# A four-layer transformer on one core: when the rows of layer 1's experts are listed and gathered, and where the first score maxima are kept

## The chip, the cores and the metric

The kernel runs on one core of one Trainium2 chip. A core has five engines with instruction streams of their own: TensorE (PE in the profile) for matmuls and transposes, VectorE (DVE), ScalarE (ACT), GpSimd (POOL), and SyncE (SP), which issues DMAs. TensorE writes into PSUM, a small memory that VectorE and ScalarE read, but GpSimd does not. The metric is the device time of one execution in microseconds (us), as the median of several runs; smaller is better.

## The reference

Four layers, each an attention and a feed-forward part, work on 16 sequences of 256 tokens, 128 features each (4096 tokens). Around each part stands a layer norm with a scale and a shift per sequence, and its output is added to the stream `x` with a gate per sequence. The change touches layer 1's feed-forward part and, by a shared routine, layer 2's attention. Layer 1's feed-forward part is itself a small transformer layer, with attention over 16 heads of 8 features and a mixture of 8 experts, of which each token uses two:

```python
def _L1_ffn_ref(src, ...):
    x = _ln(src + _attention(src, Wq, bq, Wk, bk, Wv, bv, Wo, bo), ln1_g, ln1_b)
    gates = softmax(x @ gW + gb)
    top2_scores, top2_idx = top_k(gates, 2)
    w = (one_hot(top2_idx, 8) * top2_scores[..., None]).sum(1)
    h = relu(einsum('nd,edf->enf', x, W1) + b1[:, None, :])
    y = einsum('enf,efd->end', h, W2) + b2[:, None, :]
    return _ln(x + einsum('ne,end->nd', w, y), ln2_g, ln2_b)
```

Layer 2's attention has 16 heads of 8 features too, rotary positions, and a causal mask. Both are softmax attentions: for each query the largest score is subtracted from the scores ahead of the exponential.

## The kernel before, in words

All of `x` stays in SBUF, features on partitions. Tokens are worked on in 8 blocks of 512 (two sequences).

**The attention of heads of 8** (`attend8`) is used by layer 1's feed-forward part and by layer 2's attention. A unit is one sequence; a block has two units, and a unit has `per` = 8 cycles. In a cycle TensorE makes scores of one sort for a later unit, queries by keys, from which only the maxima are taken (`Sm`, in the PSUM place `ps_max`; VectorE's reduction at L1343 reads them), and scores of the other sort for the current unit, keys by queries, of which ScalarE takes the exponential (`Se`, in `ps_exp`; L1348). Each of the two places holds one tile. The maxima run `lead` = 10 cycles ahead (`per + self.LEAD`). So in the first ten cycles of each call there are maxima and no exponentials: `live_e` is false, `ps_exp` stands unused, and each cycle's scores have to wait until VectorE has read those before. When the eight maxima of a unit are there, `less_maxima` turns them and takes them from the queries (`qm`, L1236).

The maxima use keys multiplied with a mask (`km`, L1224, two instructions on GpSimd). They are made by `start_unit`, at the end of the last cycle of the unit ahead; `mt` counts the cycles of a unit's maxima, and `mt == per - 1` is the last.

**Later work.** At the end of each cycle `self.advance()` takes one step of each generator in `self.later`. In layer 1 these are `gates(blk)`, one for each finished block. It makes the gate's softmax and then chooses: the two best experts of each token (`top1` twice) with the one-hot rows, the weights, and then `listed`. Blocks choose in groups: `{1: (0, 1), 3: (2, 3), 5: (4, 5), 6: (6,), 7: (7,)}`: block 5's generator does blocks 4 and 5 together.

**Lists.** The 4096 tokens are handled as two halves of four blocks. For each half there is an array `rows` in device memory with a list for each expert. `listed` counts, by matmuls, the place of each token in the lists of its two experts, and then for each block turns its 512 tokens to rows (`list_rows`) and writes them to their places by 8 indirect DMAs from GpSimd (128 rows of 128 numbers each, L819). With a half's last block `pieces` works out which expert each piece of 256 rows belongs to.

**Pieces.** After the attention a loop runs over 2 x 23 pieces. `fetch` loads a piece's rows and the expert's weights (L1530 and L1532, from SP's queue), `turn` turns the rows, `hidden` and `out` do the expert's two layers, and the result goes to `done` in device memory (L1564, from ScalarE's queue). Step n of the loop does `fetch(n + 2)`, `turn(n)`, `hidden(n - 1)`, `out(n - 2)` and then three times `self.advance()`. The second half's pieces read the second half's lists.

**Tails.** When the first half's results are out (step 24), `tail(0)` starts among the later work: for each block 8 indirect DMAs on GpSimd fetch both experts' results of each token back from `done` (L1476); then it yields a fixed number of steps, `9 if self.in_pieces else 4`, adds the biases by matmuls, sums the two gathered rows with their weights on VectorE (8 instructions), turns the sum back on TensorE (`sums_turned`), and ends with a layer norm and the addition to `x`. A tail starts the next one when its own gathers are issued. Two buffers serve the gathered rows, so tail 2 waits until tail 0 has summed. Tails 0 to 3 run among the second half's pieces, tails 4 to 7 in layer 2's attention.

**The order.** In these stages TensorE's instructions keep the order in which the program writes them (`self.strict`). The streams of the other engines are put in order by a planner at build time: among the instructions that it takes for ready, by its own costs and due times, it takes the one written first; what it takes for ready early may move far ahead. So memory fills that layer 2 writes stand among layer 1's list DMAs in the trace. On the chip each engine then goes through its stream in that order and waits at each instruction for what that instruction needs.

Of the kernel before, what the change touches and what calls it, by code (L numbers as in the profile page):

```python
# [9 lines left out]
F32 = mybir.dt.float32  # L10
# [221 lines left out]
class _Kernel:  # L232
    def __init__(self, ctx, tc, t, out):
        self.ctx, self.tc, self.nc, self.t, self.out = ctx, tc, tc.nc, t, out
        self.turn = 0
        self.strict = self.strict_all = False
        self.later = []
        self.in_pieces, self.listed_halves, self.tailed, self.holds = False, 0, 0, {}
        self.tails_begun = self.halves_done = self.summed = 0
        self.lists_on = False  # L240
        self.dve, self.act, self.gps = (_InOrder(self, e) for e in (tc.nc.vector, tc.nc.scalar, tc.nc.gpsimd))


# [536 lines left out]
    def listed(self, blks, src, chosen, pool):  # L780

        half, t0 = divmod(4 * blks[0], 16)
        n = 4 * len(blks)
        ts = slice(t0, t0 + n)
        H, ends = self.hots[half][:, :, ts], self.ends[half]
        ps = self.bank()
        pv = ps[:, : 8 * (n + 1)].rearrange("p (t e) -> p t e", e=8)
        self.mm(pv[:, :n], self.prefix, chosen, start=True, stop=False, skip_group_check=True)
        for t in range(n):
            self.mm(  # L790
                pv[:, t + 1 :], self.c("mean"), bc(chosen[:, t : t + 1], [P, n - t, 8]),
                start=False, stop=t == n - 1, skip_group_check=True,
            )
            if t % 4 == 3:
                yield True
        at = pool.tile([P, n, 8], F32, tag="l_at", name="l_at")
        self.dve.scalar_tensor_tensor(at, pv[:, :n], float(P), bc(ends.unsqueeze(1), [P, n, 8]), ALU.mult, ALU.add)
        self.dve.scalar_tensor_tensor(ends, pv[:, n], float(P), ends, ALU.mult, ALU.add)
        yield
        z = self.list_z[:, :, :n]  # L800
        for i in range(2):
            self.dve.tensor_mul(z[:, i], H[:, i], at)
        yield
        place = self.place[half][:, :, ts]
        self.dve.tensor_reduce(place, z, AX.X, ALU.add)
        idx = pool.tile([P, 2, n], I32, tag="l_i", name="l_i", bufs=2)
        self.dve.tensor_copy(idx, place)
        for k, blk in enumerate(blks):
            ps = self.bank()
            for t in range(4):  # L810
                self.turned(ps[:, t * P : (t + 1) * P], src[:, blk * BLK + t * P : blk * BLK + (t + 1) * P])
            yield True
            rows = self.list_rows[:, blk % 4, :]
            self.act.copy(rows, ps)
            yield
            for t in range(4):
                for i in range(2):
                    to = bass.IndirectOffsetOnAxis(ap=idx[:, i, 4 * k + t : 4 * k + t + 1], axis=0)
                    self.nc.gpsimd.indirect_dma_start(self.rows[half][:, :], to, rows[:, t * P : (t + 1) * P], None)  # L819
                    if not self.in_pieces or i:  # L820
                        yield
        if blks[-1] % 4 == 3:
            yield from self.pieces(half, pool)
# [353 lines left out]
    def attend8(self, nt, group, prepare, finish, scale, causal=False, masks=(None, None)):  # L1177
# [124 lines left out]
        for cycle in range(-lead, units * per):  # L1302
            mx, ex = cycle + lead, cycle
            mu, mt = divmod(mx, per)
            eu, et = divmod(ex, per)
            live_m, live_e = mu < units, ex >= 0
            if mx == 0:
                start_unit(0)
            mms = []
            if live_m:  # L1310
                cs, t, j0 = first[mt]
                nk = (t + 1) * P if causal else NQ
                d = U[mu]
                Sm = self.ps_max.tile([P, 1024], F32, tag="max", name="ps_max").rearrange("p (j c i k) -> p j c i k", j=2, c=len(cs), i=2)
                if qmask is not None:
                    for j in range(2):
                        o = Sm[:, j, :, :, nk - P : nk].rearrange("p c i k -> p (c i) k")
                        self.mm(o, self.ident16, bc(qmask.unsqueeze(1), [P, 2 * len(cs), P]), skip_group_check=True)
                for c in range(len(cs)):
                    for j in range(2):  # L1320
                        r = slice(32 * (j0 + j), 32 * (j0 + j) + 32)
                        mms.append((c, Sm[:, j, c, :, :nk], d["q"][r, cs[c], t * P : (t + 1) * P], d["km"][r, cs[c], :, :nk], qmask is None and c == 0))
            if live_e:
                xcs, xt, xj0 = then[et]
                q0 = xt * P if causal else 0
                e = U[eu]
                Se = self.ps_exp.tile([P, 1024], F32, tag="exp", name="ps_exp").rearrange("p (j c i q) -> p j c i q", j=2, c=len(xcs), i=2)
                if kmask is not None:
                    for j in range(2):
                        o = Se[:, j].rearrange("p c i q -> p (c i) q")  # L1330
                        self.mm(o, self.ident16, bc(kmask.unsqueeze(1), [P, 2 * len(xcs), P]), skip_group_check=True)
                for c in range(len(xcs)):
                    for j in range(2):
                        r = slice(32 * (xj0 + j), 32 * (xj0 + j) + 32)
                        mms.append((c, Se[:, j, c, :, q0:], e["k"][r, xcs[c], xt * P : (xt + 1) * P], e["qm"][r, xcs[c], :, q0:], kmask is None and c == 0))
            for c, o, lhsT, rhs, fresh in sorted(mms, key=lambda x: x[0]):
                self.mm(o, lhsT, rhs, start=fresh, skip_group_check=True)
            if live_m:

                a = self.m8[mu % 2][:, t, 8:9]  # L1340
                dims = [list(a.ap[0]), [32, 2], [2 * P, len(cs)], [P + 16, 2]]
                o = bass.AP(tensor=a.tensor, offset=a.offset + 2 * P * cs[0] + 32 * j0, ap=dims)
                nc.vector.tensor_reduce(o, Sm[:, :, :, :, :nk], AX.X, ALU.max, negate=True)  # L1343
            if live_e:
                if xj0 == 0:
                    e["E"] = self.att.tile([P, 4, len(xcs), 2, NQ], F32, tag="E8", name="E8", bufs=3)
                E = e["E"][:, xj0 : xj0 + 2, :, :, q0:]
                nc.scalar.activation(E, Se[:, :, :, :, q0:], AF.Exp, scale=scale)  # L1348
                if causal:
                    D = e["E"][:, xj0 : xj0 + 2, :, :, q0 : q0 + P].rearrange("p j c i q -> p (j c i) q")  # L1350
                    nc.gpsimd.affine_select(D, D, [[0, 4], [1, P]], ALU.is_ge, 0.0, base=0, channel_multiplier=-1)
            for f in held:
                f()
            held = []
            if live_m and mt == per - 1:
                held.append(lambda u=mu: less_maxima(u))
            if live_e and et == 0:
                held.append(lambda u=eu: values(u))
            if live_e and xj0 == 2:
                held.append(lambda u=eu, x=et, E=e["E"]: weighted(u, x, E))  # L1360
            sides = [g for g in sides if step(g)]
            self.advance()
            for g in ready.values():
                step(g)

            if live_m and mt == per - 1 and mu + 1 < units:
                start_unit(mu + 1)
        for f in held:
            f()
        for g in sides:  # L1370
# [6 lines left out]
    def layer1_ffn(self):  # L1377
# [21 lines left out]
        with ExitStack() as ctx:  # L1399
# [4 lines left out]
            def gates(blk):  # L1404
# [3 lines left out]
                yield  # L1408
                yield from self.gate_softmax(comb[:, 4 * blk : 4 * blk + 4, :], 4, 8, one)
                yield  # L1410
                blks = {1: (0, 1), 3: (2, 3), 5: (4, 5), 6: (6,), 7: (7,)}.get(blk)
                if not blks:
                    return
                n = 4 * len(blks)
# [50 lines left out]
            def tail(blk):  # L1465
# [5 lines left out]
                g = self.list_rows[:, 2 * (blk % 2) : 2 * (blk % 2) + 2, :].rearrange("p a (u i d) -> p (a u) i d", i=2, d=P)  # L1471
                wT, acc = self.h1[:8, :], sums[:, blk % 2, :]
                for t in range(4):
                    for i in range(2):
                        of = bass.IndirectOffsetOnAxis(ap=self.origin[half][:, i, t0 + t : t0 + t + 1], axis=0)
                        nc.gpsimd.indirect_dma_start(g[:, t, i], None, self.done[half][:, :], of)  # L1476
# [2 lines left out]
                self.tails_begun = blk + 1  # L1479
                if blk + 1 < 4 * self.halves_done:  # L1480
                    self.later.append(tail(blk + 1))
                for _ in range(9 if self.in_pieces else 4):
                    yield
                ps = self.bank()
                for t in range(4):
# [6 lines left out]
                for i in range(2):  # L1492
                    for t in range(4):
                        v = slice(t * P, (t + 1) * P)
                        self.dve.scalar_tensor_tensor(
                            acc[:, v], g[:, t, i], w[:, i, t0 + t : t0 + t + 1], acc[:, v] if i else ps[:, v], ALU.mult, ALU.add
                        )
                    yield
                self.summed = blk + 1
                y = self.sums_turned(acc)  # L1500
# [630 lines left out]
```

## Time and profile before

| | us |
|---|---|
| median of 3 runs (lowest to highest) | 3432.42 (3426.85 to 3433.61) |
| the profiled execution's own time | 3416.51 |
| its span, first to last instruction | 3414.8 |
| layer 1, attention of heads of 8: first maxima | from 1789.7 |
| its first exponentials' cycle | 1826.0 |
| its last exponential (L1348) begins | 2238.4 |
| first half's pieces end on TensorE | 2312.3 |
| second half's pieces on TensorE | 2339.0 to 2419.3 |
| layer 2's attention: first maxima | 2450.5 |

Busy shares of the span: PE 90%, DVE 58%, ACT 51%, POOL 37%; the mean granted TensorE clock is 0.946. In a timeline each line is one instruction, or several alike in a row (x2): start, busy time, engine, source line, operation, output from input, and in brackets how long the engine stood idle ahead of it and what ended the wait. In lists of waits a line says which engine waited at which line for which, in total, how often, and the longest.

### The profile page before, as it was taken

How to read it: one execution, taken by the hardware profiler on the slowest of the kernel's cores; microseconds unless marked ns; L12 is line 12 of the kernel's file. 1: busy time of each engine (PE TensorE's matmuls, PEld its weight loads, DVE VectorE, ACT ScalarE, POOL GpSimd, SP SyncE). 2: the span in 40 equal slices, each digit the busy share in tenths (PEclk: the TensorE clock that was granted, in tenths of full speed). 3: DMA queues.
4: the chain of work that ended last, by engine and by line, in shares of the span. 5: the costliest groups of instructions: out<-in, count | busy, mean ns of one | idle time of the engine just before them, and what ended most of it. 6: DMA issues, size and time to landing. Idle time of an engine off the chain costs nothing.

```text
span 3414.8 us, 51574 instructions
## 1 busy us (share of the span) xinstructions
PE 3058.7 (90%) x19100; PEld 1804.4 (53%) x19100; DVE 1984.0 (58%) x4602; ACT 1740.6 (51%) x4474; POOL 1271.3 (37%) x1128
## 2 busy tenths in 40 slices
PE   5999999979999999999987888886789989899887
PEld 3566666655666677767752333365434444455443
DVE  4777777744444566666654656532356675545564
ACT  3777777754222566666643544443223444575543
POOL 4777777730000233443430021124343333234355
PEclk9999999999999999999997999977789999999998
DMA  3030000000000600000000000044200000000000
GB/s 126 12 40 1 1 1 1 1 25 1 1 1 1 236 1 1 1 1 1 1 1 1 1 13 7 27 121 143 69 18 15 1 1 1 1 1 1 1 13 13
DMA packets 43178, 77.13 MB, mean 23 GB/s; under 512 B 5920, under 2 KB 22736, under 8 KB 42288
## 3 DMA queue, kind: packets, MB, share of 16 engines
q1 hardware_dynamic: 31888, 58.48, 6.0%
q0 software_dynamic: 4416, 9.33, 0.9%
q10 hardware_dynamic: 6624, 6.03, 0.5%
q8 instruction: 151, 2.47, 0.3%
q14 instruction: 99, 0.81, 0.1%
HBM read 44.69 MB, written 33.32 MB: 23 GB/s over the span
## 4 chain that ended last, share of the span: by engine, by line
PE 61%; DVE 10%; ACT 4%; POOL 4%; DMA 3%; issue 3%; POOLq 0%; DVEq 0%; SPq 0%; ACTq 0%
PE ps_one L267 21%; PE ps_big L267 14%; PE ps_out L267 9%; PE ps_max L267 7%; PE ps_one L270 7%; DVE m L1343 4%; DMA rows<-list_rows,l_i 2%; PE ps_exp L267 2%; POOL E L224 1%; ACT ln_sq L224 1%; DVE ln_xc L224 1%; PE ps_hid L267 1%; DVE pv L224 1%; ACT E L1348 1%; POOL list_rows L1476 1%
## 5 line engine op out<-in xcount | busy, mean ns | idle before, releaser
L224 POOL TENSOR_TENSOR E<-E,sm_inv 128x1024 f32<-128x1024 f32 (+1 forms) x256 | 430.0, 1680 | 480.2 <-PE ps_big L267 189.2
L1343 DVE TENSOR_REDUCE m<-ps_max 128x4 f32<-128x1024 f32 (+1 forms) x256 | 279.4, 1091 | 253.4 <-PE ps_exp L267 156.0
L1348 ACT ACTIVATE E<-ps_exp 128x1024 f32<-128x1024 f32 (+1 forms) x256 | 234.4, 916 | 361.5 <-PE ps_exp L267 283.1
L267 PE MATMUL ps_big<-h,w_f_W 128*128 128x512 f32 x768 | 359.4, 604 | 3.9 <-DVE s L982 3.9
L267 PE MATMUL ps_max<-km,q 32*128 32x512 f32 (+1 forms) x1024 | 289.1, 643 | 79.6 <-DVE m L1343 59.0
L224 ACT ACTIVATE E<-E,sm_neg 128x256 f32<-128x256 f32 x512 | 254.2, 497 | 198.6 <-DVE sm_neg L1072 198.6
L270 PEld LDWEIGHTS ps_one<-w_cst,E 128*128 128x128 f32 x1792 | 203.5, 141 | 162.4 <-POOL E L224 109.4
L267 PE MATMUL ps_exp<-qm,q 32*128 32x512 f32 (+1 forms) x1024 | 280.2, 625 | 4.4 <-ACT E L1348 4.0
L270 PE MATMUL ps_one<-w_cst,E 128*128 128x128 f32 x1792 | 243.0, 276 | 38.5 <-POOL E L224 38.1
L224 DVE COPY PT<-ps_one 128x512 f32<-128x512 f32 x320 | 209.0, 687 | 102.4 <-PE ps_one L270 101.5
L267 PE MATMUL ps_big<-kT,qT 64*128 64x256 f32 (+1 forms) x2048 | 264.9, 377 | 0.0
L267 PEld LDWEIGHTS ps_out<-w_f_W,s 128*128 128x128 f32 (+1 forms) x2048 | 188.7, 190 | 91.7 <-issue 41.2
L267 PE MATMUL ps_one<-PT,v 128*64 128x256 f32 (+1 forms) x2048 | 226.5, 364 | 1.4 <-DVE PT L224 1.0
L224 ACT ACTIVATE E<-ps_big,sm_neg 128x128 f32<-128x128 f32 (+1 forms) x512 | 208.8, 422 | 23.8 <-DVE sm_inv L224 21.8
L1072 DVE CUSTOM_DVE_ANT_0 E<-ps_big,bias 128x256 f32<-128x256 f32 x512 | 186.8, 421 | 48.4 <-PE ps_big L267 37.4
L267 PEld LDWEIGHTS ps_big<-h,w_f_W 128*128 128x128 f32 x768 | 137.4, 191 | 141.7 <-issue 119.4
L267 PE MATMUL ps_out<-w_f_W,s 128*128 128x128 f32 (+1 forms) x2048 | 201.0, 280 | 11.4 <-DVE s L1755 11.1
L224 POOL TENSOR_TENSOR r_r<-r_r,r_t 128x512 f32<-128x512 f32 x128 | 162.5, 1270 | 125.3 <-DVE r_t L224 105.2
L981 ACT ACTIVATE s<-ps_big,w_vecs 128x512 f32<-128x512 f32 x128 | 87.7, 687 | 222.5 <-PE ps_big L267 222.4
L267 PEld LDWEIGHTS ps_big<-kT,qT 64*128 64x128 f32 x2048 | 166.5, 187 | 58.0 <-issue 49.3
L982 DVE SCALAR_TENSOR_TENSOR s<-ps_big,w_vecs,s 128x512 f32<-128x512 f32 x128 | 95.9, 751 | 167.1 <-ACT s L981 167.1
L267 PEld LDWEIGHTS ps_max<-km,q 32*128 32x128 f32 x1024 | 84.0, 199 | 199.4 <-DVE m L1343 98.9
(319 smaller groups left out, 6086.7 us busy)
## 6 DMA issues: line engine op xcount, KB each, us to landing
rows<-zeros SPq DMA_DIRECT2D x8, 2048.0 KB, 18.9
list_w<-in_f_W SPq DMA_DIRECT2D x46, 257.0 KB, 3.4
list_sums<-rows SPq DMA_DIRECT2D x46, 128.0 KB, 3.0
done<-l_o ACTq DMA_DIRECT2D x46, 128.0 KB, 3.5
rb_rows<-rb_d SPq DMA_DIRECT2D x1, 4088.0 KB, 44.1
w_a_qkv<-in_a_qkv SPq DMA_DIRECT2D x2, 1536.0 KB, 8.5
w_f_W<-in_f_W SPq DMA_DIRECT2D x3, 1024.0 KB
bias<-rb_rows SPq DMA_DIRECT2D x16, 192.0 KB, 4.0
```

What stands on the lines that cost most here:

```text
L224: ins = f(*args, **kw)
L267: self.ordered(self.nc.tensor.matmul(out, lhsT, rhs, start=start, stop=stop, **kw))
L270: self.ordered(self.nc.tensor.transpose(out, in_, self.c("ident")))
L981: nc.scalar.activation(s, gv[:, :BLK], AF.Silu, bias=self.v("b1_0", c))
L982: nc.vector.scalar_tensor_tensor(s, gv[:, BLK:], self.v("b2_0", c), s, ALU.add, ALU.mult)
L1072: nc.vector.tensor_tensor_reduce(e[:, i], S[:, i], bias[g][:, i, off : off + T], 1.0, BIG, ALU.add, ALU.min, neg[:, i : i + 1])
L1343: nc.vector.tensor_reduce(o, Sm[:, :, :, :, :nk], AX.X, ALU.max, negate=True)
L1348: nc.scalar.activation(E, Se[:, :, :, :, q0:], AF.Exp, scale=scale)
L1476: nc.gpsimd.indirect_dma_start(g[:, t, i], None, self.done[half][:, :], of)
```

## The change

Five edits, in layer 1's feed-forward part and in `attend8`.

1. Blocks 4, 5, 6 and 7 each choose and list by themselves, each after its own gates; blocks 0 and 1, and 2 and 3, still do so in pairs.
2. A flag `quiet` is set in the last two cycles of each unit's maxima, ahead of the cycle's `advance`. While it is set, `listed` and `tail` issue no further indirect DMA and yield.
3. In cycles without exponentials, the scores for the maxima of every second cycle go to `ps_exp`'s place.
4. A tail among the pieces yields 20 steps, not 9, between its gathers and its sums.
5. A tail among the pieces yields two steps more between its sums and their turning.

```diff
@@ listed
                 for i in range(2):
+                    while self.quiet:
+                        yield
                     to = bass.IndirectOffsetOnAxis(ap=idx[:, i, 4 * k + t : 4 * k + t + 1], axis=0)
                     self.nc.gpsimd.indirect_dma_start(self.rows[half][:, :], to, rows[:, t * P : (t + 1) * P], None)
@@ attend8
-                Sm = self.ps_max.tile([P, 1024], F32, tag="max", name="ps_max").rearrange("p (j c i k) -> p j c i k", j=2, c=len(cs), i=2)
+                if live_e or mx % 2 == 0:
+                    Sm = self.ps_max.tile([P, 1024], F32, tag="max", name="ps_max")
+                else:
+
+                    Sm = self.ps_exp.tile([P, 1024], F32, tag="exp", name="ps_exp")
+                Sm = Sm.rearrange("p (j c i k) -> p j c i k", j=2, c=len(cs), i=2)
...
             sides = [g for g in sides if step(g)]
+
+            self.quiet = live_m and mt >= per - 2
             self.advance()
...
+        self.quiet = False
         for f in held:
             f()
@@ layer1_ffn, gates
-                blks = {1: (0, 1), 3: (2, 3), 5: (4, 5), 6: (6,), 7: (7,)}.get(blk)
+                blks = {0: None, 1: (0, 1), 2: None, 3: (2, 3)}.get(blk, (blk,))
@@ layer1_ffn, tail
                 for t in range(4):
+                    while self.quiet:
+                        yield
                     for i in range(2):
                         of = bass.IndirectOffsetOnAxis(ap=self.origin[half][:, i, t0 + t : t0 + t + 1], axis=0)
                         nc.gpsimd.indirect_dma_start(g[:, t, i], None, self.done[half][:, :], of)
...
-                for _ in range(9 if self.in_pieces else 4):
+                for _ in range(20 if self.in_pieces else 4):
                     yield
...
+                    yield
+                if self.in_pieces:
+                    yield
                     yield
                 self.summed = blk + 1
                 y = self.sums_turned(acc)
```

More of the change, by code (lines that the diff above doesn't have):

```diff
@@ L239, in __init__ @@
         self.tails_begun = self.halves_done = self.summed = 0
-        self.lists_on = False
+        self.lists_on = self.quiet = False
         self.dve, self.act, self.gps = (_InOrder(self, e) for e in (tc.nc.vector, tc.nc.scalar, tc.nc.gpsimd))
```

## The prediction

> **What bounds the kernel now.** I read the page's busy shares first: TensorE is busy 90% of the span, so time can come only from stretches where it stands still or runs at half clock. The clock by slices dips around 1790 to 1830 and 2240 to 2490 us, and the chain of work that ended last names "DMA rows<-list_rows,l_i", so I then took the waits and the engines' timelines there. Four kinds of idle time appear.
>
> First, the second half's lists. Waits from 2240 to 2430, then GpSimd's and TensorE's timelines:
>
> ```profile
> PE ps_in L270 <- DMA list_sums<-rows: 26.7, 1, 26.7
> ```
>
> ```profile
> 2255.55 0.97 POOL L819 DMA_INDIRECT rows<-list_rows,l_i  x1 [22.52 <-DVE h L1458]
> ...
> 2261.89 0.97 POOL L819 DMA_INDIRECT rows<-list_rows,l_i  x1 [0.15 <-issue]
> ...
> 2319.68 0.96 POOL L819 DMA_INDIRECT rows<-list_rows,l_i  x1 [1.53 <-DMA rows<-list_rows,l_i]
> ...
> 2334.66 0.96 POOL L819 DMA_INDIRECT rows<-list_rows,l_i  x1 [1.56 <-DMA rows<-list_rows,l_i]
> ```
>
> ```profile
> 2311.28 1.05 PE L267 MATMUL ps_out<-list_w,s 128*128 128x128 f32 x8
> 2339.03 0.66 PE L270 MATMUL ps_in<-w_cst,list_sums 128*128 128x128 f32 x2 [26.69 <-DMA list_sums<-rows]
> ```
>
> The writes of one half wait for each other, about 2.5 us apiece alone and 4 to 5 beside the pieces' loads. Blocks 5, 6 and 7 (24 writes) fall after the attention; TensorE has finished the first half's pieces and waits 26.7 us for the last of them.
>
> Second, the masked keys behind list writes, in GpSimd's, ScalarE's and TensorE's timelines:
>
> ```profile
> 2046.33 0.97 POOL L819 DMA_INDIRECT rows<-list_rows,l_i  x1 [1.55 <-DMA rows<-list_rows,l_i]
> 2047.34 2.68 POOL L1224 TENSOR_SCALAR km<-q,w_cst 128x512 f32<-128x512 f32 x4
> ```
>
> ```profile
> 2038.43 0.69 ACT L1170 ACTIVATE q<-ps_one,w_vecs 128x512 f32<-128x512 f32 x1
> ```
>
> ```profile
> 2048.74 1.22 PE L267 MATMUL ps_max<-km,q 32*128 32x512 f32 x2 [5.04 <-POOL km L1224]
> ```
>
> The keys were ready at 2039.1; the eighth write stood ahead of the mask. The same comes at 2162.22 with 5.67 us.
>
> Third, the leads of both attentions, where one PSUM place makes TensorE and VectorE take turns, and the clock over such a stretch (columns: busy time and count of PE, PEld, DVE, ACT, POOL; clock; DMA):
>
> ```profile
> 1808.35 2.08 PE L267 MATMUL ps_max<-km,q 32*128 32x512 f32 x4 [1.40 <-DVE m L1343]
> 1811.75 2.08 PE L267 MATMUL ps_max<-km,q 32*128 32x512 f32 x4 [1.33 <-DVE m L1343]
> ```
>
> ```profile
> 2466.12 0.59 PE L267 MATMUL ps_max<-half_below,ident 128*128 128x256 bf16 x2 [1.33 <-DVE m L1343]
> ```
>
> ```profile
> 1805.00:1813.00 8.00, 5.28 (x12) 1.38 (x12) 2.59 (x3) 0.00 (x0) 0.00 (x0) 0.50 0.00 0
> ```
>
> Fourth, the tails' sums, which hold TensorE and VectorE until gathered rows land:
>
> ```profile
> 2360.93 0.91 PE L270 MATMUL ps_one<-w_cst,list_sums 128*128 128x128 f32 x3 [2.36 <-DVE list_sums L224]
> ```
>
> ```profile
> 2362.92 0.35 DVE L224 SCALAR_TENSOR_TENSOR list_sums<-list_rows,list_room,list_sums 128x128 f32<-128x128 f32 x1 [1.61 <-DMA list_rows<-done,origin]
> ```
>
> **What the Trainium skill says.** "DMA: Bandwidth & Descriptors", section "Anatomy of one DMA", gives about 2.0 us plus bytes over 436e3 per us for a DMA from GpSimd, mostly the wait for the write's receipt; 64 KB would be 2.15 us by it (an estimate), and the trace has 2.24. So eight chained writes can't be shortened, only moved. "TensorE: Matmul & The Clock Gate", "Part 1: The HAM clock gate", says that the clock is halved until a window of about 3.4 us has been busy. The trace has the half clock in the leads (0.50), but three busy stretches of 6 us there stayed at half, so it does not simply agree. The same page, "Architectural detail", says that GpSimd, ScalarE and VectorE take their queues strictly in order; the mask behind the eighth write shows it.
>
> **The change part by part.**
>
> *Block 4 and block 5 apart.* By the program's cycles, block 5's chosen lists are written where block 4's are now (2214 to 2234), and block 4's 16 cycles sooner, beside block 3's, which go to another array and aren't waited for. So 16 writes remain after the attention. Block 6's can't begin before its places (VectorE's l_i at 2261.35) and rows (ScalarE, 2260.49), so about 2261.9, where the third of today's 24 starts. With today's spacing the sixteenth is the one at 2319.68; it lands 2.23 later, at 2321.9, against 2336.9: **15 us** less. Bounds: 8 if block 5's writes spill out of the attention, 22 if fewer writes space closer. TensorE then still waits some 11.7 us. Cost: 19 more small VectorE instructions (13 to choose, 6 to place) at 0.19, less 19 x 0.035 for the narrower ones: 2.9 us, in cycles where TensorE waits for VectorE anyway by 1.3 to 1.7 us. I take 2, from 0 to 4. TensorE's counting matmuls are about as many as before.
>
> *Later sums.* From 2352.76 to 2402.66, 49.9 us, TensorE does ten pieces of 1.975 (19.75) and the four tails' own work, 4 x 3.56 (turns 0.44 + 0.45, biases 0.95, norm 2 x 0.86): 14.2. Some **16 us** are waits and half clock. Counted from the half's start (2339.03), the gathers begin at 10.75 and follow every 1.26; the eighth landed at 23.9. With 20 steps tail 0's biases come after ten pieces, at 13.73 + 4 x 1.975 + 1.5 = 23.1, its turn at about 26.5: no wait. Tail 1 is only 4 steps behind: biases near 27.5, while its last gather starts at 10.75 + 15 x 1.26 = 29.6 and lands 4.3 later; VectorE's sums then stand ahead of a piece's copy for some 5 us. Tails 2 and 3 come 20 us later and find their rows landed. So about 11 of 16 return; one is lost again, because tail 3 now ends with the last pieces (turn at step 62 of 72, last addition at 69) and layer 2's first norm is behind it. Net **10**, from 2 to 15. GpSimd issues the same 32 gathers (40 us).
>
> *Maxima in two places.* Waits on VectorE in layer 1's lead: 1.33, 1.74, 1.40, 1.33, 1.33, 1.42 and 1.33, of which I keep all but the last (the first exponentials share the place): 8.5. In layer 2's: 0.79 twice and 1.33 four times: 6.9. Together 15.4. With the waits gone TensorE is busy throughout, and if the clock rises, a cycle costs VectorE's 1.28 instead of 2.08: 5 us more in each lead. I add 4: **19**, from 8 to 29. What is late next is VectorE, with a norm (2.8 us) among its reductions.
>
> *Quiet.* Block 1's and block 3's rows are turned two cycles (about 7 us) later, since the eight writes ahead of them are held for two cycles. The planner put eight writes into the 10.5 us between rows and keys; into the 3 us left it puts two or three, ended by about 2043.5, when TensorE asks. So 5.04 + 5.67, plus 1.9 each for matmuls at half clock after the stall (1.22, 1.06, 1.97 for 0.70, 0.59, 1.09): 14.4; VectorE absorbs part: **10**. The held writes come after the keys, hidden by the rest of the unit. If the planner still puts all eight ahead, they end some 7.5 later and the part costs 15. In layer 2 tail 7's gathers move behind the masks at 2518, a stall of 3.93; but what moves may hold back the causal selection on GpSimd (4.39 at 2497). I take 2, from -4 to 4.
>
> Sum: 15 + 10 + 19 + 10 + 2 - 2 = 54, less 2 for a shift in what the planner does elsewhere: **52 us**. On the profiled execution that is 3416.5 - 52 = 3364.5; its time lies 15.9 under the median of the runs, so I take the difference from the median: **3380**.
>
> **The rivals.**
>
> *The planner ignores quiet* (12 in 100). Only the order of writing changes, and the planner is free on GpSimd. For it: writes of cycles 70 to 73 already stand ahead of a mask written in cycle 69. Against: the rows' turning on TensorE is pinned, and it moves. Then -15 instead of 10: gain 27, **3405**.
>
> *Transfers take the place of the lists' wait* (10). The second half starts sooner, but gathers and loads collide: landings took up to 4.8 us against 2.2. Lists and tails bring 9 instead of 25: gain 36, **3396**.
>
> *The clock rises in both leads* (8). For it: no gap is left. Against: the 6 us stretches at half clock. The other 6 to 10 come: **3370**.
>
> *No change that can be measured* (3): what is won is waited for elsewhere, **3432**.
>
> *Slower by the planner's order* (5). A reduction set behind other VectorE work costs TensorE 1.3 us, as at 1843.55 and 1850.16 (1.41, 1.32). If the new order of the two attentions' 256 cycles adds such a wait, it decides from 52 / 1.3 = 40 cycles on; at 55 it is 72 - 52 = 20 slower, **3452**. Against: the order within a steady cycle is not touched.
>
> **How the numbers follow.** The forecast has 62 in 100, with 3365 to 3396 of its own. The range reaches from the clock's case past the planner's: 3355 to 3412, which leaves out the two cases without gain and about 10 of the rest. About 0.2% (7 us) is what a measurement here can tell from no change. Faster is 62 + 12 + 10 + 8 = 92, same 3, slower 5.
>
> **What would show it.** Right: only 16 list writes after the last exponentials; TensorE's wait ahead of the second half near 12 us, not 26.7; no 5 us wait for km; no wait on m in the leads; the second half's pieces within about 70 us instead of 80.3. Wrong: list writes still eight in a row ahead of km, or a new wait of VectorE for gathered rows as long as the old ones, or the leads no shorter.

## The result, and the profile after

The kernel after takes 3385.1 us (median of four runs, 3373.2 to 3396.3) against 3432.2 for the kernel before on the same chip: a ratio of 0.9865, 95% interval 0.9826 to 0.9904. The forecast was 3380, 5 us lower, with 52 us to be gained where 47 were (33 to 60 by the interval). The profiled execution took 3379.59 us. The stages, each measured from event to event (us); the last column is a later trace of the same kernel after, from group 2 of the experiments, and is needed because one row of the first trace is disturbed:

| stage | before | after | after, later trace |
|---|---|---|---|
| start to first maxima of layer 1 | 1789.7 | 1786.8 | 1783.6 |
| lead 1: first maxima to first exponential | 38.4 | 23.5 | 23.5 |
| first to last exponential of layer 1 | 410.3 | 407.6 | 407.6 |
| last exponential to the second half's first turn | 100.6 | 83.1 | 82.0 |
| second half's pieces, to layer 2's first norm | 80.3 | 104.9 | 73.1 |
| that norm to layer 2's first maxima | 31.2 | 31.4 | 31.6 |
| lead 2 | 35.0 | 20.0 | 19.3 |
| first to last exponential of layer 2 | 429.4 | 418.6 | 422.7 |
| the rest | 499.9 | 502.1 | 500.6 |
| span | 3414.8 | 3377.9 | 3344.0 |

First, the lists. TensorE's waits from 2220 to 2420 of the kernel after (who waited, for whom, total, times, longest), then GpSimd's and TensorE's timelines:

```profile
PE ps_in L270 <- DMA list_sums<-rows: 8.9, 1, 8.9
```

```profile
2241.92 0.98 POOL L821 DMA_INDIRECT rows<-list_rows,l_i  x1 [4.10 <-issue]
...
2293.95 0.97 POOL L821 DMA_INDIRECT rows<-list_rows,l_i  x1 [1.53 <-DMA rows<-list_rows,l_i]
2296.48 0.97 POOL L821 DMA_INDIRECT rows<-list_rows,l_i  x1 [1.55 <-DMA rows<-list_rows,l_i]
```

```profile
2290.92 1.05 PE L267 MATMUL ps_out<-list_w,s 128*128 128x128 f32 x8
2300.86 0.66 PE L270 MATMUL ps_in<-w_cst,list_sums 128*128 128x128 f32 x2 [8.89 <-DMA list_sums<-rows]
```

Sixteen writes are left after the attention, the last at 2296.5, and the wait ahead of the second half is 8.9 us instead of 26.7.

Second, the masked keys, in GpSimd's and TensorE's timelines. Three writes stand ahead of the next unit's two mask instructions, the rest behind, and the scores that use the new keys wait 0.35 us, not 5.04, and for VectorE. Between the first and the last exponential of layer 1 no wait for masked keys is left:

```profile
2026.27 0.96 POOL L821 DMA_INDIRECT rows<-list_rows,l_i  x1 [1.54 <-DMA rows<-list_rows,l_i]
2027.26 1.36 POOL L1226 TENSOR_SCALAR km<-q,w_cst 128x512 f32<-128x512 f32 x2
2028.79 1.01 POOL L821 DMA_INDIRECT rows<-list_rows,l_i  x1 [0.17 <-issue]
```

```profile
2029.86 0.70 PE L267 MATMUL ps_max<-km,q 32*128 32x512 f32 x2 [0.35 <-DVE m L1350]
```

Third, the leads. All of TensorE's waits for VectorE's reductions (m) in lead 1 and in lead 2, and a stretch of lead 1 (columns as before: busy time and count of PE, PEld, DVE, ACT, POOL; clock; DMA):

```profile
1797.62 1.13 PE L267 MATMUL ps_exp<-km,q 32*128 32x512 f32 x4 [1.28 <-DVE m L1350]
1799.39 1.13 PE L267 MATMUL ps_max<-km,q 32*128 32x512 f32 x4 [0.65 <-DVE m L1350]
...
1809.04 1.13 PE L267 MATMUL ps_exp<-qm,q 32*128 32x512 f32 x4 [1.32 <-DVE m L1350]
...
2448.30 0.38 PE L267 MATMUL ps_max<-half_below,ident 128*128 128x256 bf16 x2 [0.53 <-DVE m L1350]
```

```profile
1794.00:1802.00 8.00, 6.06 (x23) 1.79 (x22) 7.12 (x9) 1.32 (x2) 0.00 (x0) 0.91 0.00 0
```

Scores now alternate between `ps_exp` and `ps_max`; four matmuls take 1.13 us instead of 2.08 for part of the lead, and VectorE is busy 7.12 of 8 us.

Fourth, the pieces with the tails: here the trace goes against the forecast, 104.9 us where 70 were expected. From its timeline of all engines:

```profile
2317.28 0.38 PE L270 MATMUL ps_in<-w_cst,list_sums 128*128 128x128 f32 x2
2317.59 0.95 POOL L1488 DMA_INDIRECT list_rows<-done,origin  x1 [0.30 <-issue]
2318.85 0.95 POOL L1488 DMA_INDIRECT list_rows<-done,origin  x1 [0.30 <-issue]
2320.11 0.95 POOL L1488 DMA_INDIRECT list_rows<-done,origin  x1 [0.30 <-issue]
2321.34 0.37 ACT L1577 COPY l_o<-ps_out 128x256 f32<-128x256 f32 x1 [4.89 <-remote]
...
2321.38 0.42 DVE L1555 COPY l_x<-ps_in 128x256 f32<-128x256 f32 x1 [7.42 <-remote]
```

By the profile TensorE had turned a piece's rows by 2317.7, and had ended the results that ScalarE is to copy before that; yet VectorE and ScalarE go on together at 2321.3, by a release that the profile can't name ("remote"). GpSimd alone goes on. The same comes six times between 2317 and 2366. Whether the later sums bring this, or something outside the change, was the first question for the runs.

### The profile page after: what moved, and what is told of

The parts are those of the page before. It is cut to its first block, busy times and chain, and to the rows that moved or that the text cites. A ratio compares the mean times of both kernels' runs of the same rounds, so it can differ in the third digit from the quotient of the medians.

```text
span 3377.9 us, 51611 instructions
## 1 busy us (share of the span) xinstructions
PE 3038.7 (90%) x19102; PEld 1797.5 (53%) x19102; DVE 1984.9 (59%) x4622; ACT 1741.1 (52%) x4474; POOL 1272.1 (38%) x1128
## 5 line engine op out<-in xcount | busy, mean ns | idle before, releaser
L1350 DVE TENSOR_REDUCE m<-ps_max 128x4 f32<-128x1024 f32 (+1 forms) x246 | 268.6, 1092 | 204.3 <-PE ps_exp L267 146.8
L267 PE MATMUL ps_max<-km,q 32*128 32x512 f32 (+1 forms) x984 | 266.4, 618 | 57.8 <-DVE m L1350 51.9
L267 PE MATMUL ps_out<-w_f_W,s 128*128 128x128 f32 (+1 forms) x2048 | 201.8, 281 | 10.4 <-DVE s L1770 10.1
L267 PEld LDWEIGHTS ps_big<-kT,qT 64*128 64x128 f32 x2048 | 166.6, 187 | 58.0 <-issue 49.3
L267 PEld LDWEIGHTS ps_one<-PT,v 128*64 128x64 f32 x2048 | 133.4, 138 | 79.6 <-DVE sm_inv L224 14.9
```

The source lines that it names most:

```text
L267: self.ordered(self.nc.tensor.matmul(out, lhsT, rhs, start=start, stop=stop, **kw))
```

## The experiments

Ratios are to the kernel before, whose runs are shared by the kernels of one group. The groups ran on different chips, so times are compared within a group.

### Group 1: each part undone in the kernel after

**The kernel after again** (no edit).

> The kernel after, once more, for its spread and for a second trace of the second half's pieces. Theory A (stretches of 3 to 4 us in which TensorE, VectorE, ScalarE and SP all stand while GpSimd goes on issuing gathers belong to this kernel): the pieces of the second half, from their first turn to layer 2's first norm, again take 95 to 110 us, and the stretches again lie within the two bursts of 16 gathers. Theory B (they were an accident of one execution): 70 to 80 us, no such stretch, and a time near 3355. Ratio to the kernel before by A 0.986, by B below 0.982.

Measured: 3353.5 us (3351.3 to 3360.5), before 3401.1, ratio 0.9861 (0.9847 to 0.9875). The pieces took 73.65 us, with no wait for "remote". Theory B of the two held for the pieces, but not for the ratio: the kernel before is lower here too, by 31 us.

**Tails as before.**

```diff
-                for _ in range(20 if self.in_pieces else 4):
+                for _ in range(9 if self.in_pieces else 4):
                     yield
...
-                if self.in_pieces:
-                    yield
-                    yield
```

> The kernel after, but a tail among the pieces yields 9 steps between gathers and sums, and none after them, as in the kernel before. Theory A (the later sums are the loss: they hold back the buffers, so that tail 2's gathers come in a second burst, and each burst brings its stalls): the second half's pieces go back to about 80 us from 105, and the time falls by 15 to 25, to about 3362. Rival (the later sums brought the 10 us forecast and the stalls have another cause, such as the earlier start of the half): the pieces take 110 us or more and the time rises to about 3395.

Measured: 3358.5 us (3356.6 to 3364.8), ratio 0.9871 (0.9857 to 0.9886), 5.1 above the kernel after. Theory A is wrong: the kernel after has its later sums and no stalls on this chip, and without them the time rose. The rival had the sign right and the size wrong. Edits 4 and 5 went together here, so what each does alone isn't shown. The second half's window in this kernel, with its waits for the gathered rows' sums, and then that of the kernel after:

```profile
2299.67:2378.88 79.21, 70.98 (x422) 59.56 (x423) 29.26 (x75) 38.09 (x88) 36.27 (x36) 0.93 0.62 180
```

```profile
PE ps_one L270 <- DVE list_sums L224: 5.8, 3, 3.8
```

```profile
2300.03:2373.68 73.65, 68.78 (x423) 58.88 (x423) 27.49 (x72) 37.70 (x88) 34.47 (x35) 0.94 0.65 194
```

With later sums that wait is gone from the list, and the half is 5.6 us shorter.

**Lists in pairs as before.**

```diff
-                blks = {0: None, 1: (0, 1), 2: None, 3: (2, 3)}.get(blk, (blk,))
+                blks = {1: (0, 1), 3: (2, 3), 5: (4, 5), 6: (6,), 7: (7,)}.get(blk)
```

> The kernel after, but blocks 4 and 5 choose as a pair, as in the kernel before. Theory (the lists apart bring what the wait ahead of the second half lost): 24 list writes after the attention instead of 16, TensorE's wait there back from 8.9 to about 27 us, time 13 to 18 higher, about 3400. Rival (what the wait loses comes back as stalls in the pieces, because the half starts earlier against the same transfers): the pieces of the second half shorten by as much as the wait grows, time within 5 us of the kernel after.

Measured: 3356.1 us (3351.6 to 3356.7), ratio 0.9862 (0.9848 to 0.9877), only 2.6 above. The gap ahead of the second half, from turn to turn, was back at 27.3 us from 10.6, but the pieces were hardly shorter (72.8 against 73.65), so the rival's mechanism is wrong as well. The loss was made up earlier: first to last exponential took 395.3 us against 405.5. Until block 4's gates TensorE and VectorE do the same in both kernels, and still the two part before that. One instruction of the pairs, then the same one of the kernel after:

```profile
1939.73 0.70 PE L267 MATMUL ps_max<-km,q 32*128 32x512 f32 x2 [1.64 <-DVE m L1350]
```

```profile
1944.15 1.22 PE L267 MATMUL ps_max<-km,q 32*128 32x512 f32 x2 [1.65 <-DVE m L1350]
```

After the same wait the clock stays up in one and is halved in the other. Whether that was the pairs' doing or chance went to group 2. It isn't where most of the time goes, though: 92 exponentials after the first the two are 1.1 us apart (291.4 and 292.5 us), and 9.7 of the 10.2 are lost in the next 28.

**Without quiet.**

```diff
-            self.quiet = live_m and mt >= per - 2
+            self.quiet = False
```

> The kernel after, but the flag is never set, so list writes and tail gathers are issued in every cycle. Theory (quiet keeps the masked keys from standing behind eight list writes): stalls of about 5 us for km at two block ends of layer 1 are back, and about 4 in layer 2; time 8 to 15 higher, about 3397. Rival (the flag mostly moves the writes to where something else waits for them; first to last exponential of layer 1 took 407.6 us after and 410.3 before, only 2.7 less): time within 5 us of the kernel after, although the km stalls are back.

Measured: 3368.0 us (3358.0 to 3375.6), ratio 0.9895 (0.9877 to 0.9913), 14.5 above, as the theory had it. But the six runs fall into two groups, three of 3358 to 3362 and three of 3374 to 3376 (the trace is of the latter), so the 14.5 stands between some 6 and some 21. First to last exponential of layer 1 took 421.1 us against 405.5, and TensorE's waits there have the keys again:

```profile
PE ps_max L267 <- POOL km L1226: 9.6, 2, 5.0
```

The other 6 of those 15.6 us are no wait of its own: TensorE's clock is lower (mean 0.92 against 0.94 from first to last exponential). About 2 of them are not the stalls': after 48 exponentials the two traces stand at 148.5 and 146.5 us, ahead of the first stall. The kernel after's first trace and its later one, with 407.6 us, have 148.5 and 148.6 there too; against them the stretch is 13.5 us longer, 6.6 by the first stall and 6.9 by the second. In layer 2 one wait for keys is back, of 3.9 us, and TensorE waits 4.4 us for GpSimd's causal selection (E); the kernel after's four traces have none for keys there, but 7.2 to 9.6 for E. The whole stretch took 423.7 us, inside the 416.3 to 427.8 of the traces with quiet, so a gain there isn't shown.

### Group 2: maxima, pairs and lists once more

**One place for the maxima.**

```diff
-                if live_e or mx % 2 == 0:
+                if True:
                     Sm = self.ps_max.tile([P, 1024], F32, tag="max", name="ps_max")
```

> The kernel after, but all first maxima go to the one PSUM place again. Theory (two places bring the leads' gain): layer 1's lead, from the first maxima to the first exponential, goes back from 23 to 26 us to about 38, layer 2's from 20 to 30 us back to 35; time 17 to 25 higher than the kernel after. Rival (part of it is only moved, because VectorE and the clock set the next cycles anyway): both leads longer as said, but the attentions behind them shorter; time within 8 us.

Measured: 3376.9 us (3371.5 to 3380.3), before 3404.6, ratio 0.9923 (0.991 to 0.9937); 22.4 above the kernel after of this group. Lead 1 is 38.5 us and lead 2 37.1, while the attentions behind them are as long as with two places (405.8 and 417.8; 405.5 to 407.6 and 416.3 to 423.2 in the kernel after's traces). The theory holds.

**Pairs again** (the edit above).

> The kernel after with blocks 4 and 5 as a pair, a second time. In its first trace layer 1's attention, from first to last exponential, took 395.3 us and kept the full clock, against 405.5 with the lists apart, where the clock halved after one wait of 1.65 us for VectorE that both have. Theory (the lists apart cost that clock, whatever the execution): again about 395 us, mean clock near 0.960, time equal to the kernel after within 5 us although TensorE waits 27 us ahead of the second half. Rival (the halving is chance in one execution): 400 to 410 us in this trace, and time 10 to 15 higher than the kernel after.

Measured: 3364.5 us (3360.0 to 3367.1), ratio 0.9882 (0.9867 to 0.9897), 10.1 above the kernel after. First to last exponential took 400.0 us, and the mean clock over the span was 0.954, as the rival had it: the full clock of the first trace was chance to a good part (92 exponentials after the first this trace stands at 296.0 us, that one at 291.4).

**The kernel after, third trace.**

> The kernel after, a third trace, beside the pairs. If the lists apart cost the clock: first to last exponential of layer 1 again 404 to 409 us, mean clock near 0.956. If it is chance: anything from 395 to 409. No stretches in which all engines but GpSimd stand, and pieces of 73 to 75 us in the second half, if those of the first trace were an accident; 95 or more if not.

Measured: 3354.5 us (3345.7 to 3359.2), ratio 0.9862 (0.9847 to 0.9877); 407.6 us from first to last exponential, pieces 73.1, no "remote". This trace and that of the pairs above run evenly for 92 of the 128 exponentials (294.5 and 296.0 us from the first), and then part: the 120th is at 386.5 with the lists apart and 381.6 with pairs, so 6.3 us are lost in these 28 cycles. The stretch with pairs and then apart, with TensorE's wait for VectorE in each:

```profile
2104.28:2189.93 85.65, 72.92 (x568) 30.78 (x569) 48.73 (x78) 42.18 (x58) 13.04 (x15) 0.95 0.09 27
```

```profile
PE ps_max L267 <- DVE m L1350: 11.0, 12, 1.7
```

```profile
2101.63:2193.60 91.97, 76.84 (x574) 32.66 (x570) 51.56 (x96) 42.67 (x58) 21.87 (x24) 0.91 0.11 32
```

```profile
PE ps_max L267 <- DVE m L1350: 14.3, 14, 1.9
```

VectorE has 18 instructions and 2.8 us more, TensorE waits 3.3 us more for it, and is 3.9 us longer busy at a lower clock.

More than half of the 6.3 us is lost in the first four of the 28 cycles (pairs, then apart):

```profile
2104.28:2115.27 10.99, 8.27 (x76) 3.16 (x77) 6.28 (x7) 4.68 (x5) 0.97 (x1) 0.94 0.02 7
```

```profile
2101.63:2116.29 14.66, 10.12 (x76) 3.91 (x72) 7.67 (x14) 4.63 (x5) 0.97 (x1) 0.77 0.02 7
```

With the lists apart, small instructions of block 4's choice stand on VectorE just ahead of a reduction; TensorE waits 4.5 us for reductions, not 2.7, and then does the same 76 matmuls in 10.12 us, not 8.27. This repeats: in the ten traces with the lists apart these four cycles take 14.5 to 15.1 us at a clock of 0.77, in the four with pairs 10.6 to 12.2 at 0.86 to 1.00.

**The lists alone**, in the kernel before:

```diff
-                blks = {1: (0, 1), 3: (2, 3), 5: (4, 5), 6: (6,), 7: (7,)}.get(blk)
+                blks = {0: None, 1: (0, 1), 2: None, 3: (2, 3)}.get(blk, (blk,))
```

> The kernel before with one edit: blocks 4 to 7 choose each by itself. Forecast of the prediction: the wait ahead of the second half 26.7 us down to about 12 and the time 13 lower (ratio 0.996). Theory from the second comparison (what the wait gives, the attention takes, by clock or by work): the wait falls to about 9, first to last exponential grows by 10 to 15 us, ratio 0.998 to 1.001.

Measured: 3396.0 us (3384.3 to 3401.4, 15 runs) against 3404.6, ratio 0.9974 (0.9965 to 0.9983): 8.6 us gained, between the two expectations. The wait is 8.3 us. Against the first trace of the kernel before, 92 exponentials run evenly again (298.4 and 299.0) and the 120th is at 394.8 against 388.9: 6.5 us, as above. The second trace of the kernel before, in group 3, takes 2.8 us longer than its first over the same 28 (92.7 against 89.9), so of the 6.5 only 3.7 are clear of what differs between executions.

### Group 3: where the standing stretches belong

**The kernel before again** (no edit).

> The kernel before itself, for a trace of it from a chip on which its runs are 28 to 31 us below those of the first pair, so that the stages can be compared with the later traces. If the first pair's offset was in stretches in which all engines but GpSimd stand, this trace has none and its second half's pieces again take about 80 us; first to last exponential of layer 1 about 408 to 411 us, the wait ahead of the second half about 27. Ratio 1.000 within the interval.

Measured: 3424.3 us (3421.4 to 3429.8), ratio 0.9996 (0.9988 to 1.0005). The expectation's premise fell: on this group's chip the kernel before takes about 3425, not 3400. And its trace has the stretches. The second half's window, and one wait of ScalarE in it:

```profile
2328.33:2431.41 103.08, 80.10 (x423) 65.86 (x423) 28.80 (x75) 37.89 (x88) 35.90 (x36) 0.79 0.49 137
```

```profile
2370.73 0.84 ACT L1550 ACTIVATE s<-ps_hid,list_w 128x256 f32<-128x256 f32 x2 [22.06 <-remote]
```

The pieces of the kernel *before* take 103.1 us here, where they took 80.3 in its first trace. So the stretches are not a product of the change.

**Gathers behind the first masked keys**, a further edit to the kernel after, aimed at the rotation's wait that both kernels have at the start of layer 2's attention:

```diff
             if mx == 0:
                 start_unit(0)
+                if self.halves_done == 2 and self.tails_begun == 4:
+                    slots = self.list_rows.rearrange("p a (u d) -> p (a u) d", d=P)[:, :, :1]
+                    nc.gpsimd.tensor_copy(slots, U[0]["km"][:, 0, 0, :16].unsqueeze(2))
```

> The kernel after with one more edit: at the start of layer 2's attention GpSimd copies a number of the first masked keys into each slot of the gathered rows, so that the 16 gathers of tails 4 and 5 can't be issued ahead of the rotation's additions and the first masks. Theory (those gathers, 20 us of GpSimd, cause the 8 us wait of TensorE for the rotation in front of layer 2's first scores): that wait falls to 1 or 2 us, the stretch from layer 2's first norm to its first maxima from 31.5 to about 24, and with TensorE warm the lead takes about 20 us in more executions instead of 20 or 30; time 6 to 16 lower than the kernel after, about 3344, ratio 0.982 to 0.984. Rival (the gathers then stand ahead of what comes next on GpSimd, the masks of the second unit and the causal selection): waits of TensorE for these of 5 us or more in the lead and behind it, time within 4 us of the kernel after.

Measured: 3380.5 us (3370.9 to 3384.5), before 3425.7 on this chip, ratio 0.9872 (0.9857 to 0.9887). From the norm to the first maxima 22.3 us, so the mechanism works; but no gain in the ratio. The pieces took 105.8 us, with "remote" waits as in the other trace from this chip.

### Group 4: the further edit beside the kernel after

First the kernel with the edit just shown, then the kernel after as it is:

> The kernel with the gathers of tails 4 and 5 behind the first masked keys, again, beside the kernel after on the same chip. Its first trace has the stretch from layer 2's first norm to its first maxima at 22.3 us (31.5 in the kernel after), but waits of 6.3 us for masked keys and 3.2 for the subtracted queries in the lead, and its ratio to the kernel before was 0.9872 against 0.9861 and 0.9862. Theory (the 9 us are worth their time, the first ratio came from stalls of the chip): 6 to 10 us below the kernel after here. Rival (they are lost again in the lead and behind it): within 4 us of it.

> The kernel after beside it. If this chip is one with stretches in which all engines but GpSimd stand (runs of the kernel before near 3425 us): the second half's pieces take 95 to 110 us; if it is one without (near 3402): 73 to 75 us. Ratio to the kernel before 0.986 in either case.

Measured: 3349.8 us (3339.5 to 3352.9), ratio 0.9845 (0.9824 to 0.9866), with the edit; 3351.0 (3340.8 to 3365.4), ratio 0.986 (0.9836 to 0.9885), for the kernel after; before 3400.3. They can't be told apart: the medians fit the rival, but runs that spread over 13 and 25 us don't exclude the theory's 6. The pieces took 73.1 us in both, no "remote". TensorE's waits ahead of the first maxima in the kernel after, and in the lead and the cycles behind it with the edit:

```profile
PE ps_one L267 <- DVE rot_t L1677: 6.9, 1, 6.9
```

```profile
PE ps_out L267 <- POOL E L1361: 7.0, 3, 3.6
PE ps_max L267 <- POOL km L1226: 4.8, 2, 3.5
```

The kernel after has, in the same lead and cycles:

```profile
PE ps_out L267 <- POOL E L1358: 8.8, 3, 4.4
PE ps_max L267 <- POOL km L1226: 3.3, 1, 3.3
```

The 6.9 us are gone with the edit, and norm to maxima is 23.4 us against 31.7. The longer wait for keys, 3.5 us, is that of the first maxima, which the kernel after has too; only the other, 1.3 us for the second unit's keys, is new. Together these waits are 11.8 us with the edit and 12.1 without, so it isn't they that take the gain back. Yet layer 2's attention takes 427.8 us against 423.2 and the rest 499.9 against 497.0; whether that is the edit's doing isn't shown.

## Why the prediction was right, and where its steps were off

Undone one at a time, the parts cost, against the kernel after of the same group:

| part | forecast | measured |
|---|---|---|
| maxima in two places | 19 | 22.4 |
| quiet, both layers | 12 | 14.5 |
| later sums | 10 | 5.1 |
| lists apart, with their cost on VectorE | 15 - 2 = 13 | 2.6 and 10.1; alone 8.6 |

The first three and the mean of the two for the lists, 6.4, add up to 48.4; the whole change gains 47.1, 47.6, 50.1 and 49.3 us in the first pair and in groups 1, 2 and 4. With intervals of about 0.0014 to each ratio, a single entry is good to some 7 us and the sum of four to about 13; within that the parts add. Later sums alone, 5.1, is not clear of this by its time; it rests on the 5.6 us of its stage. The forecast's sum of 52 is 2 to 5 too high: two terms were too large by about 11 together, two too small by about 6, and it had taken off 2 for what the planner does elsewhere. That the sum comes so near is in part luck, since these errors cancel.

*Maxima in two places.* Right in kind and nearly in size. Lead 1 went from 38.5 to 23.5 or 25.6 us (forecast 8.5 and a share of the clock's 4). The forecast's "would show it" had no wait on VectorE left; in the first trace three remain in lead 1, and VectorE, with reductions of 1.22 us and the next block's norm among them, is busy for 7.12 of 8 us. The step had named it as what is late next. The rival of a clock that rises in both leads is what the first trace shows (0.71 and 0.87, against 0.50 and 0.54 before), but not every one: in its four traces lead 2 of the kernel after took 20.0, 30.0, 19.3 and 22.3 us, against 35.0 in the kernel before and 37.1 with one place. By the leads of the traces the part is worth 20 us where lead 2 takes 30.0 us and 33 where it takes 19.3; the 4 us that the forecast added lie between these two kinds of execution.

*Quiet.* Right: three writes ahead of the mask, no stall. The planner didn't ignore the flag, which was the first rival. In the trace without it layer 1's attention is 13.5 us longer than in the kernel after's traces that begin like it, against 10: 9.6 of waits and 3.9 at a lower clock. That is near the 14.4 of the forecast's own sum; that VectorE would absorb part of it isn't seen. The 2 for layer 2 didn't come: the wait for keys went, and the selection on GpSimd was held back for about as long, which the forecast had named. Between before and after the stretch is only 2.7 us shorter (410.3 and 407.6) because the lists, next, put back much of what quiet takes off.

*Lists apart.* The wait fell by 17.8 us, not 15. But the cost was put at 2, "in cycles where TensorE waits for VectorE anyway": that step failed. A cycle in which TensorE already waits for VectorE has no slack on VectorE: 2.8 us more of its work gave 3.3 us more of wait and, with the clock, 6.3 us. That the clock falls over the wait is read from the traces, ten with the lists apart against four with pairs; no run separates the two. In the traces of the two pairs, beside the kernel after of their groups, the stretch ahead of the second half is 16.2 and 16.9 us longer, the 28 cycles are 9.7 and 6.3 shorter and the pieces 0.8 and 2.0. That leaves 5.7 and 8.6 for the lists apart, beside the 2.6 and 10.1 of the medians. So the rival that transfers collide in the pieces accounts for 2 us at most: undisturbed, these take 73 us, and 71 to 73 with pairs.

*Later sums.* The mechanism is right, the size half. The waits for gathered rows, 5.8 us, are gone. The forecast let 11 of 16 us return, but those 16 were a remainder: the stretch less priced matmuls. The waits recorded for TensorE in the half of the kernel before came to only 8.3 us (6.0 for the sums, 1.0, 0.9 and 0.4 for others), and 4.7 are still there (2.3 and 1.5 for ScalarE, 0.9). Nor did tail 1's sums wait 5 us for their rows. The rest of the 5.6 us by which the half shrank, about 2, is TensorE's own busy time (70.98 and 68.78 us). The failing step is to have taken a remainder for idle time without holding it against the list of waits.

*What would show it.* In the kernel after the half came to 73.1 to 73.65 us where "about 70" was said, in the undisturbed traces; the first trace's 104.9 would have spoken against the step, and wrongly.

## What to carry to other kernels

Work that is added to an engine on which another already waits was paid in full here, and more where TensorE's clock fell over it; a term "hidden in the wait" has to name an engine with time to spare. Size a gain from the recorded waits, not from what is left of a stretch after pricing its matmuls. And when one stage of one trace contradicts the forecast, take a second trace, of both kernels if possible, before explaining it: here the stage was 31 us longer in the first trace, and on another chip 23 us longer for the kernel before as well.

## What the runs showed of the hardware

**A half clock that busy TensorE doesn't leave.** Two windows, each holding lead 2 of the kernel after: first from its trace in group 1, then from that in group 2.

```profile
2405.30:2435.25 29.95, 29.95 (x93) 12.40 (x93) 13.76 (x21) 2.52 (x4) 2.27 (x3) 0.50 0.00 1
```

```profile
2401.38:2420.70 19.32, 18.30 (x93) 8.11 (x94) 13.14 (x20) 2.52 (x5) 1.69 (x3) 0.91 0.00 1
```

The instructions are the same 93. In one TensorE is busy by the profile for 29.95 us without a gap at 0.50; in the other its matmuls run at full clock from 3.6 us after the start (2401.38 to 2404.96). The Trainium skill, "TensorE: Matmul & The Clock Gate", section "Part 1: The HAM clock gate", has the clock rise after at least one busy window of about 3.4 us. The second trace agrees with it, the first does not, and the measurement decides: being busy was not enough. What is needed besides, the runs don't tell. The difference is 10 us in one lead alone, between executions of one kernel; in the eight traces with two places and without the further edit, lead 2 took 19.3 to 22.3 us in three and 28.3 to 30.0 in five. The halving after the same 1.65 us of wait, in group 1, is of this kind too.

**Stretches in which only GpSimd goes on.** In the second half's pieces, TensorE, VectorE, ScalarE and SP stood for 3 us and more at a time (12 us for VectorE, 22 for ScalarE at most), for releases that the profile doesn't name, while gathers were issued every 1.26 us. They were in three traces, of three kernels, one of them the kernel before. Against the undisturbed traces the pieces were longer by 31 us (104.9 against 73.65), 23 (103.1 against 80.3) and 33 (105.8 against 73.1). On the chip where that kernel was traced again, its runs lie near 3425 us, and on the three chips without them at 3400 to 3405. The first pair's chip belongs with the former by its runs, though its trace of the kernel before has none. The same gathers at the same spacing brought nothing in ten traces on the other chips, so the gathers alone aren't the cause; what it is stays open, as no run took it apart.
